# A unit's first value matmuls, one division piece and one background piece moved by half a step

## The chip, the cores and the metric

The kernel runs on one core of a Trainium2 chip. The metric is the device time of one execution in microseconds; the median of several runs is compared. The engines are named as in the profile: PE (TensorE matrix multiplies; PEld its weight loads), DVE (VectorE), ACT (ScalarE), POOL (GpSimd) and SP (SyncE, which issues the transfers).

## The reference

A decoder layer on x of 2 x 2048 x 512 in float32: self-attention of 16 heads of 32 with rotary positions, then attention to a context with a gelu in place of the softmax, then a feed-forward step with the signs of its weights, each after a layer norm and each added to x.

```python
def reference(x, ctx_1024, W_q, W_k, W_v, W_o, weights, scale, bias):
    def attn(x):
        Q, K, V = apply_rope(proj(W_q)), apply_rope(proj(W_k)), proj(W_v)
        scores = jnp.einsum('bhqd,bhkd->bhqk', Q, K) / jnp.sqrt(jnp.float32(DK))
        out = jnp.einsum('bhqk,bhkd->bhqd', jax.nn.softmax(scores, axis=-1), V)
        return out.transpose(0, 2, 1, 3).reshape(b, s, D) @ W_o.T
    def xattn(x, w1, w2):
        return jax.nn.gelu(x @ w1.T, approximate=True) @ w2
    def ffn(x):
        return jnp.clip((x @ sign(weights).T) * scale + bias, -100, 100)
    x = x + attn(_layernorm(x))
    x = x + xattn(_layernorm(x), ctx_1024, ctx_1024)
    x = x + ffn(_layernorm(x))
    return x
```

## The kernel before, in words

The two batches are worked through one after the other. For each, `project_batch` makes queries, keys and values, and `Attention.run` then does the attention, in which nearly all of the time goes by.

**Units and steps.** A unit is 256 queries of a group of four heads; a batch has 32 units (`NU`), and a block of 512 queries has eight of them. A unit has eight steps (`STEPS`), each over two of the 16 chunks of 128 keys, and a step has two half-steps: in the first, heads 0 and 1 are scored (`heads`) while the row maxima of heads 2 and 3 (`others`) are made for a unit eleven steps ahead (`AHEAD`); in the second the pairs change places.

**One half-step on each engine.** PE writes the scores of two heads, transposed, into their `st` banks (`scores`, L603; eight records a half-step, since each float32 matmul shows as two passes), and the scores for the maxima into two of the `ps` banks (`maxima`, L484; four records). A step's `st` is built on that of the step before: what is added is the product with the difference of two key blocks, so each head has one `st` bank for a whole unit. ACT makes the exponentials `pw` (L744), POOL adds those of the two key chunks to `sm` (L746), and DVE takes the row maxima out of `ps` (L496). At a unit's first step `lower` (L584) sets the `st` banks to the negated maxima first.

**Values and totals, one and two steps late.** `first_half` and `second_half` belong to the step before. `weigh` (L621) multiplies the `pw` of one key chunk with the values into the bank `acc`, eight records for four heads; `total` (L635) sums `sm` of the step before that into the same bank, eight records for half the queries. In step 0 of a unit the last values and totals of the unit before are made; the second half-step there also sums the last `sm`, for all 256 queries. In step 1 there are no totals. `ps_acc` has one bank, so the first `weigh` of a unit, at step 1, writes the bank that the unit before has used.

**The division** (`divide`) is a generator, one piece for each call of `finish`: a copy of `acc` to `num` by ACT (L649), at step 0's second half-step; the reciprocal of the first 128 totals by DVE (L655); the product of these by POOL (L658) and the second reciprocal; the second product. After the last piece of a block's last unit, `after_attention` is put into `queue` for that block.

**Background work.** `after_attention` is a generator of the output projection (L394), the context attention and the feed-forward step of one block. `background(1)` runs one piece at the end of each second half-step; `background(1, light=True)`, at each odd step's first half-step, runs one only if the piece is not marked heavy (a piece with matmuls or transposes). In a batch's last four units a piece is run in each first half-step, light or not. The background's PSUM tiles come out of `ps_s`.

**What sets the order.** In `run` the instructions of PE, DVE, ACT and POOL stay in the order in which the source issues them (`manual_schedule`); waits are put where tiles are shared. PSUM has eight banks: four in `ps_t` (the `st` of four heads), three in `ps_s` (the `ps` tiles in turn), one in `ps_acc`. DMAs of a unit's maxima go out on SP's queue and are not touched.

Of the kernel before, what the change touches and what calls it, by code (L numbers as in the profile page):

```python
# [36 lines left out]
def decoder_layer(  # L37
# [35 lines left out]
    def load_x(b, ch, pool=xpool):  # L73
        t = pool.tile([P, D], F32, tag="x", name=f"x_{b}_{ch}")
        nc.sync.dma_start(t, tokens(x[b], ch))
        return t
# [89 lines left out]
    def chunk_norm(ahead, b, ch, engine=nc.gpsimd):  # L166
        xc = ahead.pop(0)
        stats = stats_tile(1)
        chunk_stats(xc, stats[:, 0, 0:2])
        y, off = scale_and_shift(engine, stats)  # L170
        yield
        xn = work.tile([P, D], F32, tag="w", name="xn")
        nc.scalar.activation(xn, xc, AF.Identity, bias=off, scale=y)
        if ch + 2 < NCH:
            ahead.append(load_x(b, ch + 2))
        yield xn
# [5 lines left out]
    def turn(xn):  # L182
        pt = ps_t.tile([P, ND, P], F32, tag="t", name="pt")
        for i in range(ND):
            nc.tensor.transpose(pt[:, i, :], xn[:, i * P : (i + 1) * P], ident)  # L185
        xnt = work.tile([P, ND, P], F32, tag="w", name="xnt")
        nc.scalar.copy(xnt, pt)
        return xnt
# [243 lines left out]
    def background(n, light=False):  # L432
        while queue and n > 0 and not (light and heavy[0]):
            more = next(queue[0], queue)
            if more is queue:
                queue.pop(0)
                heavy[0] = False
            else:
                heavy[0] = more
                n -= 1  # L440
# [16 lines left out]
    class Attention:  # L457
# [227 lines left out]
        def run(self):  # L685
            prev = None
            sums_due = None
            ends = []

            def finish():  # L690
                while ends and next(ends[0], ends) is ends:
                    ends.pop(0)

            def first_half():
                if prev is not None:
                    self.weigh(prev, 0)
                if sums_due is not None:
                    self.total(sums_due, slice(0, P))

            def second_half():  # L700
                nonlocal sums_due
                if prev is not None:
                    self.weigh(prev, 1)
                if sums_due is not None:
                    self.total(sums_due, slice(P, HQ))
                sums_due = prev
                if prev is not None and prev[1] == STEPS - 1:
                    self.total(prev, slice(0, HQ))
                    ends.append(self.divide(prev[0]))
                    sums_due = None  # L710

            ordered = tc.manual_schedule(
                engines={
                    mybir.EngineType.PE,
                    mybir.EngineType.DVE,
                    mybir.EngineType.Activation,
                    mybir.EngineType.Pool,
                }
            )
            ordered.__enter__()  # L720
            attending.append(True)
            more = self.b + 1 < B
            for t in range(NU * STEPS):
                u, i = divmod(t, STEPS)
                if t == NU * STEPS - AHEAD:
                    free.append(True)
                if more and t == (NU - 1) * STEPS:
                    self.x_next = [load_x(self.b + 1, 0), load_x(self.b + 1, 1)]
                if more and t == NU * STEPS - STEPS // 2:
                    next_norm = chunk_norm(self.x_next, self.b + 1, 0)  # L730
                    next(next_norm)
                if more and t == NU * STEPS - 2:
                    xn = next(next_norm)
                pw = big.tile([P, 4, 2, HQ], F32, tag="s", name="pw")
                sm = sums.tile([P, 4, HQ], F32, tag="sm", name="sm")
                for heads, others in (((0, 1), (2, 3)), ((2, 3), (0, 1))):
                    if i == 0:
                        self.lower(u, heads)
                        self.wrap_around(self.units[u][1])
                    self.scores(u, i, heads, 0)  # L740
                    reduce = self.maxima(t + AHEAD, others)
                    self.scores(u, i, heads, 1)
                    for h in heads:
                        nc.scalar.activation(pw[:, h], self.st[h], AF.Exp, scale=SCALE)  # L744
                    hs = slice(heads[0], heads[1] + 1)
                    nc.gpsimd.tensor_add(sm[:, hs, :], pw[:, hs, 0, :], pw[:, hs, 1, :])  # L746
                    if reduce:
                        reduce()
                    if heads[0] == 0:
                        first_half()  # L750
                        finish()
                        if u >= NU - ND:
                            background(1)
                        elif t % 2 == 1:
                            background(1, light=True)
                    else:
                        finish()
                        second_half()
                        if prev is not None and prev[1] == STEPS - 1:
                            finish()  # L760
                        if (t + AHEAD) % STEPS == 0 and u + 1 < NU:
                            self.turn_maxima(u + 1)
                        if (t + AHEAD) % STEPS == STEPS - 1 and u + 1 < NU:
                            self.split_maxima(u + 1)
                        background(1)
                prev = (u, i, pw, sm)
            xnt = turn(xn) if more else None
            first_half()
            second_half()
            while ends:  # L770
                finish()
            attending.clear()
            free.clear()
            ordered.__exit__(None, None, None)
            return xnt
# [65 lines left out]
```

## Time and profile before

| what | us |
| --- | --- |
| median of three runs | 2694.99 (2693.69 to 2695.18) |
| the profiled execution | 2694.35 |
| its span, first to last instruction | 2692.6 |
| PE busy | 2666.4 (99%) |
| PEld busy | 1475.8 (55%) |
| POOL busy | 1762.9 (65%) |
| DVE busy | 1718.6 (64%) |
| ACT busy | 1323.3 (49%) |
| L496 row maxima, 2048 | 1309.1 in all, 0.682 each |
| L655 reciprocals, 128 | 120.6 in all, 0.943 each |
| L649 copies of `acc`, 64 | 37.6 in all, 0.587 each |

The attention of the first batch runs from 216 us to about 1326, that of the second from 1549 to about 2642. A unit without background work takes 30.91 us. The granted clock of PE is full in nearly all of the span.

A line of the timeline gives the start, the time until the last of the merged instructions ends, engine, line and operation, tiles (written <- read), shape and count, and in brackets how long the engine was idle before and what released it. Matmuls are pipelined and their ends are modelled: a PE that waits in the middle of a half-step can show as busy throughout, so their starts are what is to be compared.

### The profile page before, as it was taken

The numbers are of one execution on the slowest core, as the hardware profiler recorded it, in microseconds if no ns is written. First come the engines' busy times: TensorE is split into PE (matmuls) and PEld (weight loads), VectorE is DVE, ScalarE is ACT, GpSimd is POOL, SyncE is SP. The second block draws the span as 40 slices with busy tenths as digits, with TensorE's granted clock in tenths as the row PEclk, the third lists the DMA queues.
The fourth block names the chain that finished last, engine by engine and source line by source line (L and its number), as shares of the span: only waits on it lengthen the run. The fifth ranks groups of instructions, "written<-read, shape, count | busy, mean of one in ns | idle before, by whom it ended". The sixth has DMA issues, their size and how long they took to land.

```text
span 2692.6 us, 70762 instructions
## 1 busy us (share of the span) xinstructions
PE 2666.4 (99%) x30500; PEld 1475.8 (55%) x30500; DVE 1718.6 (64%) x2928; ACT 1323.3 (49%) x2394; POOL 1762.9 (65%) x1916
## 2 busy tenths in 40 slices
PE   8999999999999999999999999999999999999998
PEld 4445555555555555555554455555555555555555
DVE  3447777667766766676344477766767667766754
ACT  2214555455546554555422155555555455546553
POOL 3227777577857786777543287766787577857782
PEclk9999999999999999999999999999999999999999
DMA  3010000000000000000201000000000000000000
GB/s 126 24 32 2 3 2 2 2 2 18 18 2 2 10 26 2 2 10 25 76 24 40 5 2 3 2 3 2 2 26 10 2 2 18 18 2 2 18 18 17
DMA packets 36824, 40.65 MB, mean 15 GB/s; under 512 B 19206, under 2 KB 19718, under 8 KB 36512
## 3 DMA queue, kind: packets, MB, share of 16 engines
q1 hardware_dynamic: 36512, 36.14, 4.5%
q8 instruction: 239, 3.92, 0.6%
q14 instruction: 73, 0.60, 0.1%
HBM read 27.23 MB, written 8.90 MB: 13 GB/s over the span
## 4 chain that ended last, share of the span: by engine, by line
PE 98%; DVE 1%; DMA 0%; issue 0%; ACT 0%; SPq 0%; POOL 0%; POOLq 0%; ACTq 0%
PE st L603 24%; PE acc L621 22%; PE ps L484 18%; PE acc L635 8%; PE po L394 4%; PE pk L195 4%; PE pq L195 4%; PE pv L195 4%; PE pf L375 2%; PE st L584 2%; PE pt L357 1%; PE po L420 1%; PE ptqk L203 1%; PE ph L401 1%; PE pt L185 1%; DMA wk<-in_wk_t_dram 0%
## 5 line engine op out<-in xcount | busy, mean ns | idle before, releaser
L746 POOL TENSOR_TENSOR sm<-pw 128x512 f32<-128x512 f32 x1024 | 1297.9, 1274 | 567.4 <-ACT pw L744 563.1
L496 DVE TENSOR_REDUCE mx<-ps 128x1 f32<-128x512 f32 x2048 | 1309.1, 682 | 500.2 <-PE ps L484 498.3
L744 ACT ACTIVATE pw<-st 128x512 f32<-128x512 f32 x2048 | 1113.2, 596 | 942.0 <-PE ps L484 733.8
L484 PE MATMUL ps<-k,q 32*128 32x512 f32 x4096 | 1192.5, 639 | 1.5 <-DVE mx L496 1.5
L621 PE MATMUL acc<-pw,v 128*32 128x256 f32 x8192 | 655.0, 391 | 0.0
L635 PE MATMUL acc<-sm,ones 128*32 128x128 f32 x7680 | 388.3, 280 | 0.0
L621 PEld LDWEIGHTS acc<-pw,v 128*32 128x32 f32 x8192 | 161.9, 108 | 405.3 <-issue 386.9
L484 PEld LDWEIGHTS ps<-k,q 32*128 32x128 f32 x4096 | 356.8, 183 | 25.2 <-issue 13.7
L635 PEld LDWEIGHTS acc<-sm,ones 128*32 128x32 f32 x7680 | 247.2, 110 | 153.9
L603 PE MATMUL st<-q,dkk 32*128 32x256 f32 x2048 | 291.0, 400 | 0.0
L603 PE MATMUL st<-q,dkv 32*128 32x256 f32 x2048 | 289.9, 400 | 0.0
L603 PE MATMUL st<-q,dkq 32*128 32x256 f32 x2048 | 289.9, 400 | 0.0
L603 PEld LDWEIGHTS st<-q,dkk 32*128 32x128 f32 x2048 | 175.0, 184 | 89.5 <-issue 51.4
L603 PEld LDWEIGHTS st<-q,dkq 32*128 32x128 f32 x2048 | 172.7, 184 | 80.0 <-issue 54.2
L603 PEld LDWEIGHTS st<-q,dkv 32*128 32x128 f32 x2048 | 174.7, 184 | 58.9 <-issue 26.4
L231 POOL TENSOR_TENSOR r<-r 128x512 f32<-128x512 f32 x64 | 81.2, 1268 | 162.4 <-DVE r L230 150.6
L655 DVE RECIPROCAL num<-num 128x128 f32<-128x128 f32 x128 | 120.6, 943 | 54.2 <-ACT num L649 54.2
L603 PE MATMUL st<-q,wrap 32*128 32x256 f32 x1024 | 144.9, 400 | 0.0
L603 PE MATMUL st<-q,k 32*128 32x256 f32 x1024 | 133.2, 375 | 0.0
L149 DVE BATCH_NORM_STATS2 st<-x 128x6 f32<-128x512 f32 x96 | 65.4, 686 | 93.6 <-DMA x<-in_x_dram 93.2
L195 PE MATMUL pk<-wk,xnt 128*128 128x512 f32 x256 | 118.1, 605 | 3.4 <-DMA wk<-in_wk_t_dram 2.0
L394 PE MATMUL po<-wo,q 128*128 128x512 f32 x256 | 117.4, 603 | 0.0
(114 smaller groups left out, 1953.8 us busy)
## 6 DMA issues: line engine op xcount, KB each, us to landing
x<-in_x_dram SPq DMA_DIRECT2D x64, 256.0 KB
out_dram<-x SPq DMA_DIRECT2D x32, 256.0 KB
mrow<-rows SPq DMA_DIRECT2D x496, 0.8 KB
wk<-in_wk_t_dram SPq DMA_DIRECT2D x2, 1024.0 KB
wq<-in_wq_t_dram SPq DMA_DIRECT2D x2, 1024.0 KB
wv<-in_wv_t_dram SPq DMA_DIRECT2D x2, 1024.0 KB
wo<-in_wo_t_dram SPq DMA_DIRECT2D x1, 1024.0 KB
wf<-in_wf_t_dram SPq DMA_DIRECT2D x1, 1024.0 KB
```

Of the source, the lines that this page charges most:

```text
L149: nc.vector.bn_stats(st, xc)
L195: nc.tensor.matmul(dst, xnt[:, i, :], w[:, i, :], start=(i == 0), stop=(i == ND - 1))
L231: nc.gpsimd.tensor_add(r[:, 0, a], r[:, 0, a], r[:, 1, a])
L394: nc.tensor.matmul(ps, ot[:, i, cols], wo[:, i, :], start=(i == 0), stop=(i == ND - 1))
L484: nc.tensor.matmul(ps, self.q[qb][self.rows[h], g, q0 : q0 + P], self.k[kb][self.rows[h], g, :], start=True, stop=True,)
L496: nc.vector.tensor_reduce(mx[:, qc, h, kb : kb + 1], ps, AX.X, ALU.max)
L603: nc.tensor.matmul(self.st[h][:, c, :], keys[r, g, kc * P : (kc + 1) * P], self.q[qb][r, g, hf * HQ : (hf + 1) * HQ], start=False, stop=Tr ...
L621: nc.tensor.matmul(acc[self.rows[h], 0, :], self.v[self.chunk(i, c)][:, d0 : d0 + DK], pw[:, h, c, :], start=(i == 0 and c == 0), stop=(i ...
L635: nc.tensor.matmul(acc[self.rows[h], 1, part], ones, sm[:, h, part], start=False, stop=(i == STEPS - 1), skip_group_check=True,)
L655: nc.vector.reciprocal(num[:, 1, part], num[:, 1, part])
L744: nc.scalar.activation(pw[:, h], self.st[h], AF.Exp, scale=SCALE)
L746: nc.gpsimd.tensor_add(sm[:, hs, :], pw[:, hs, 0, :], pw[:, hs, 1, :])
```

## The change

At step 1 of each unit (`i == 1`) three things move. The value matmuls of the unit's first key chunk (`first_half`, which has no totals there) are issued in the second half-step, just ahead of those of the second chunk, and no longer in the first. The piece of the division that stood in the first half-step (the first reciprocal) is run in the second, and so each later piece half a step later than before. The light background piece of that first half-step is left out, and the queue goes on at the next place; in a batch's last four units, the piece in the first half-step stays.

```diff
                     if heads[0] == 0:
-                        first_half()
-                        finish()
+                        if i != 1:
+                            first_half()
+                            finish()
                         if u >= NU - ND:
                             background(1)
-                        elif t % 2 == 1:
+                        elif t % 2 == 1 and i != 1:
                             background(1, light=True)
                     else:
                         finish()
+                        if i == 1:
+                            first_half()
                         second_half()
```

## The prediction

> **What bounds the kernel now.** I read the page first, above all the shares of the chain that ended last; then the list of waits, and then the timelines of TensorE (PE) and VectorE (DVE) over one change of unit, since what the change moves lies there alone.
>
> ```profile
> PE 98%; DVE 1%; DMA 0%; issue 0%; ACT 0%; SPq 0%; POOL 0%; POOLq 0%; ACTq 0%
> PEld acc L621 <- ACT num L649: 17.7, 52, 0.3
> ```
>
> First line: the chain is PE's. The second is the wait behind which the moved values stand: the first value matmul (L621) of a unit needs the one `acc` bank, which ScalarE's copy (L649) gives free. It is 0.3 us at its longest and 17.7 us over 52 times, so 0.34 us each; but L621 stands idle for "issue" as long where no copy runs (386.9 us over 968 times, 0.40 each). It is what PE needs between score matmuls and value matmuls in any case, and I price this wait at nothing.
>
> I name half-steps by the step in the unit and a (heads 0, 1) or b (heads 2, 3); one begins at its first L603. PE in a change of unit without background work, with 1a at 718.61, 1b at 720.25, 2a at 722.15, 2b at 724.37 and 3a at 726.37:
>
> ```profile
> 718.61 0.48 PE L603 MATMUL st<-q,dkk 32*128 32x256 f32 x2
> ...
> 719.68 0.64 PE L621 MATMUL acc<-pw,v 128*32 128x256 f32 x8
> 720.25 0.48 PE L603 MATMUL st<-q,dkk 32*128 32x256 f32 x2
> 720.27 0.96 PE L484 MATMUL ps<-k,q 32*128 32x512 f32 x2
> ...
> 721.06 0.59 PE L484 MATMUL ps<-k,q 32*128 32x512 f32 x1
> 721.58 0.64 PE L621 MATMUL acc<-pw,v 128*32 128x256 f32 x8
> 722.15 0.48 PE L603 MATMUL st<-q,dkq 32*128 32x256 f32 x2
> ...
> 724.37 0.48 PE L603 MATMUL st<-q,dkq 32*128 32x256 f32 x2
> ...
> 726.37 0.48 PE L603 MATMUL st<-q,dkv 32*128 32x256 f32 x2
> ```
>
> DVE in the same stretch, the maxima (L496) and the two reciprocals (L655):
>
> ```profile
> 719.78 1.29 DVE L496 TENSOR_REDUCE mx<-ps 128x1 f32<-128x512 f32 x2 [1.11 <-PE ps L484]
> 720.99 0.94 DVE L655 RECIPROCAL num<-num 128x128 f32<-128x128 f32 x1
> 721.85 1.22 DVE L496 TENSOR_REDUCE mx<-ps 128x1 f32<-128x512 f32 x2
> 722.98 0.94 DVE L655 RECIPROCAL num<-num 128x128 f32<-128x128 f32 x1
> 723.84 1.22 DVE L496 TENSOR_REDUCE mx<-ps 128x1 f32<-128x512 f32 x2
> ```
>
> Elsewhere in the loop a half-step with totals takes 1.86 and 1.90 in turn. Without totals (1a) it takes 1.64. So 1b (1.90) is 0.26 over, 2a (2.22) 0.36 and 2b (2.00) 0.14: 0.76 us a unit of waits that "PE busy 99%" hides. Their cause is the `ps` banks: there are three, so the second L484 pair of a half-step waits until the first maximum of the half-step before is out. In 1b: the first maximum runs 719.78 to about 720.47 (a maximum has 0.68), the second bank is written from some 0.06 later, its second pass is at 721.06, and L621 comes 0.52 after that. In 2a and 2b the reciprocals have pushed the maxima back.
>
> The last view is the start of a batch, where no values exist yet and score half-steps follow one another:
>
> ```profile
> 219.55 0.59 PE L484 MATMUL ps<-k,q 32*128 32x512 f32 x1
> 220.06 0.71 PE L621 MATMUL acc<-pw,v 128*32 128x256 f32 x8
> ```
>
> ```profile
> 217.07 3.79 DVE L496 TENSOR_REDUCE mx<-ps 128x1 f32<-128x512 f32 x6 [1.23 <-PE ps L484]
> ```
>
> The three half-steps there begin at 216.12, 217.09 and 217.89: a half-step of scores alone costs PE 0.97 at most. But the maxima go on in a row, and the first L621 comes at 220.06, 2.17 after the start of its half-step where 1.07 is usual. What PE gains by leaving values out, it waits for at the banks.
>
> **The change part by part.**
>
> Wait on the copy: 0, from above.
>
> First values to 1b. 1a now costs 0.97, so 1b begins at about 719.59. Its second bank still waits for the maximum that starts at 719.78, because neither L484 nor L496 of 1a moves. The bank is free at 720.53 as before and L621 of 1b comes at 721.58 as before: the 0.66 gained in 1a is all waited for. Then eight L621 more follow. Their price: the last half-step of a unit's totals has eight 256-column L635 more than its neighbour, and 0.76 us (717.85 to 718.61) against 0.33 (715.88 to 716.21) from the first L635 to the next score; so +0.43. 2a begins at 722.58, not 722.15: **+0.43**. Queued behind L484's wait on PE are 1b's later scores, both value blocks and all that follows; ScalarE's exponentials wait for those scores, but end well ahead of the next use of their scores.
>
> Here two rules of the Trainium skill pull apart. "TensorEngine Tiling (Array Packing)", Tiling Modes, says that changing the tiling mode drains the array; one change less between scores and values speaks for the change, and by it alone the unit would gain about 0.1. "TensorE: Matmul & The Clock Gate", Part 2, says that matmuls stay in program order and only weight loads are pulled ahead; by it the values cannot pass the waiting L484, and the batch's start shows just that.
>
> First reciprocal to 1b, second to 2a. Maxima follow one another at 0.61, a reciprocal follows its maximum by 0.60, and the next maximum follows a reciprocal by 0.86 (720.99 to 721.85). In 1b the first maximum can start at 720.99, the second at about 721.69 (its bank's end), the reciprocal at 722.28 until 723.2. 2a's maxima are due 1.17 after 2a begins, 723.75: nothing is late. 2a takes 1.86, 2b begins at 724.44 and takes 1.90, as usual. The second reciprocal runs from 724.95; 2b's maxima, due at 725.61, start at 725.81 and the first ends at 726.44. 3a begins at 726.34 and its second bank waits until 726.49 instead of 726.36: +0.14. 3b begins at 728.34, before at 728.22; and 3b then has the shorter of the two turns. I take **+0.08** (0.02 to 0.15) for such a unit: +0.43, less the 0.36 and 0.14 of waits in 2a and 2b, plus 0.14 in 3a, and 0.01 to round.
>
> Where work in 1b hid the second reciprocal, nothing comes back. In the unit at 503.89 a projection (L394) from 511.58 takes 3.6 us, and 2a and 2b take 1.86 and 1.90 already: +0.43 + 0.14, and about 0.05 since the chunk statistics after 2b's maxima come later: **+0.6**. With four transposes (L357) in 1b, as in the unit at 539.24 (2a there is 2.22, 2b 1.86): +0.43 - 0.36 + 0.14 = **+0.2**.
>
> Light piece at 1a. Only three pieces in each query block of 512 find themselves there in quiet units; the rest of the time the next piece is heavy, or only waits its turn. They go to the next slots. The block's pieces end in the 15th unit, before the next block's first comes in the 17th: cost 0. If that slack were gone, a piece would cost what it costs elsewhere, so PE's work is the same. The moved scale-and-shift on POOL has a cover of a whole step, since totals use `sm` one step later. The divided queries (L658) are a half-step later; their first reader is a projection a step on. No DMA moves on SP's queue.
>
> By units: 37 without PE work at 1a to 2b, 37 x 0.08 = 3.0; 12 with a projection or context matmul in 1b, 12 x 0.6 = 7.2; 6 with transposes, 6 x 0.2 = 1.2; seven at the batches' ends, about +0.4 together (four at +0.2, two at -0.2 where no maxima are left, one at 0); the first unit of each batch, where 2a's wait of 0.25 goes and 2a begins no later, 2 x -0.2 = -0.4. Sum **+11.4**. The profiled execution took 2694.35 (span 2692.6), 0.6 under the median of 2694.99; +11.4 on either gives 2705.8 or 2706.4: **2706**. Its own bounds: 0.02 and 0.15 in the 37, half and one and a half in the 18 with background: +4 to +18, 2699 to 2713.
>
> **Rivals.**
>
> *The bank wait goes (faster).* If 1b's second bank were free when 1b begins, L621 would come at 719.59 + 1.07 = 720.66, and 2a 1.0 later, at 721.66: 0.49 before today's. With 2a and 2b free of waits the quiet unit gains 0.9, those with background 0.35: 37 x 0.9 + 18 x 0.35 = 40 us, 2655. It decides where 1a's first maximum ends before 719.6. For it: the drain rule and the short 1a. Against: that maximum starts at 719.78.
>
> *The reciprocals still push (slower).* If 2a and 2b keep their waits in spite of the longer 1b, the 0.43 is lost whole in 62 units: +27 us, 2721. For it: DVE has 2 x 0.94 us to place. Against: 2a's maxima come half a microsecond after the first reciprocal's end.
>
> *It cancels.* If units with background cost no more than quiet ones, 62 x 0.05 = 3 us: 2698, which is no change. For it: a projection of 3.6 us could hide some of the 0.43. Against: PE itself does both, one after the other.
>
> **How the numbers follow.** Forecast 0.62, cancelling 0.18, reciprocals 0.10, bank wait gone 0.10. A measurement here tells about 0.2%, 5.4 us, from no change. Of the forecast's 0.62 some 0.12 lies under that; of cancelling 0.16 is no change and 0.02 faster. So faster 0.12, same 0.28, slower 0.60. The range goes from 2695 to 2718: below it most of the first rival and a little of the third, above it most of the second.
>
> **What would show it.** In the timeline: 1a at 0.97, then L484's second pair of 1b at the same distance from the first maximum as now; sixteen L621 in a row; 2a at 1.86, 2b at 1.90, 3a near 2.00; a unit's length up by under 0.15 where quiet and by 0.5 to 0.6 with a projection in 1b. Wrong, if L621 of 1b comes earlier than 2.97 after 1a's start, if 2a stays over 1.9, or if the background pieces run into the next block.

## The result and the profile after

| | before | after |
| --- | --- | --- |
| median of eight runs, us | 2694.47 (2693.69 to 2695.18) | 2702.65 (2700.66 to 2704.77) |
| the profiled execution | 2694.35 | 2704.77 |
| its span | 2692.6 | 2703.0 |

The changed kernel is slower by 8.2 us, a ratio of 1.003 with a 95% interval of 1.0019 to 1.0041. It does the same work: 30500 matmul records, 2928 on DVE, 2394 on ACT and 1916 on POOL in both.

PE in the changed kernel at the change of unit that the prediction showed, now with 1a at 719.45 and 2a at 723.41; the columns are start, duration, engine, line, operation, tiles, shape, count:

```profile
719.45 0.48 PE L603 MATMUL st<-q,dkk 32*128 32x256 f32 x2
...
720.20 0.38 PE L603 MATMUL st<-q,dkk 32*128 32x256 f32 x2
720.41 0.59 PE L484 MATMUL ps<-k,q 32*128 32x512 f32 x1
720.42 0.60 PE L603 MATMUL st<-q,dkk 32*128 32x256 f32 x4
720.84 1.21 PE L484 MATMUL ps<-k,q 32*128 32x512 f32 x2
721.37 0.70 PE L603 MATMUL st<-q,dkk 32*128 32x256 f32 x4
721.89 0.59 PE L484 MATMUL ps<-k,q 32*128 32x512 f32 x1
722.41 1.07 PE L621 MATMUL acc<-pw,v 128*32 128x256 f32 x16
723.41 0.48 PE L603 MATMUL st<-q,dkq 32*128 32x256 f32 x2
...
725.27 0.48 PE L603 MATMUL st<-q,dkq 32*128 32x256 f32 x2
...
727.17 0.48 PE L603 MATMUL st<-q,dkv 32*128 32x256 f32 x2
```

1b begins at 720.42, only 0.97 after 1a. Its later scores start at 721.37, 0.95 after its first; 1a's last two start 0.75 after its first (719.45 to 720.20). L621 comes at 722.41: 2.96 after 1a by the rounded rows, which is where it was before (718.61 to 721.58, 2.97). Then there are sixteen in a row, and 2a begins 1.00 later and not 0.57. The row at 720.84 merges a record of the first maximum's matmul with the first of the second's, which shows best among the weight loads (PEld); in the brackets stand how long PEld was idle before and what released it:

```profile
721.36 0.18 PEld L484 LDWEIGHTS ps<-k,q 32*128 32x128 f32 x1 [0.74 <-DVE mx L496]
```

What stops 1b is on DVE:

```profile
720.62 2.60 DVE L496 TENSOR_REDUCE mx<-ps 128x1 f32<-128x512 f32 x4 [1.11 <-PE ps L484]
723.13 0.94 DVE L655 RECIPROCAL num<-num 128x128 f32<-128x128 f32 x1
724.58 1.29 DVE L496 TENSOR_REDUCE mx<-ps 128x1 f32<-128x512 f32 x2 [0.51 <-PE ps L484]
725.79 0.94 DVE L655 RECIPROCAL num<-num 128x128 f32<-128x128 f32 x1
726.65 1.22 DVE L496 TENSOR_REDUCE mx<-ps 128x1 f32<-128x512 f32 x2
```

1a's first maximum starts at 720.62, 1.17 after 1a as before, and is out some 0.7 later; until then 1b has only one free bank. Since PE now stands still long enough for it to show, the list of waits names the cause (us in all, times, longest us), before and after:

```profile
PEld ps L484 <- DVE mx L496: 7.0, 10, 1.6
```

```profile
PEld ps L484 <- DVE mx L496: 50.9, 70, 1.6
```

The list after also puts 44.3 us of L621's waits, 60 times, down to the exponentials (L744). In the unit shown that is not what L621 waits for: the last exponential before it ends at 721.85, and L621 comes 0.56 later, but 0.52 after the last L484 (721.89), as it did before (721.06 to 721.58). A kernel below, the faster of the two without 1a's maxima, has 43.6 us of the same waits, and there the change gains.

Half-steps of a quiet unit, from the starts of their first L603:

| | 1a | 1b | 2a | 2b | 3a | 3b | sum |
| --- | --- | --- | --- | --- | --- | --- | --- |
| before | 1.64 | 1.90 | 2.22 | 2.00 | 1.86 | 1.90 | 11.52 |
| after | 0.98 | 2.99 | 1.86 | 1.90 | 2.00 | 1.86 | 11.59 |

Summed over the units of both attention loops the trace after is 8.6 us longer: 3.9 in the first batch, 4.7 in the second. The remaining 1.9 us of the span lie in the projections and the tail. In the profiles of the kernels below this remainder goes from -1.0 to +1.5 (the one that is equal to the kernel before in its loops has 1.3), so I don't count it to the change; the medians differ by 8.2.

### The profile page after: what moved, and what is told of

Same layout as the page of the kernel before. It is cut to its first block, busy times and chain, and to the rows that moved or that the text cites. A ratio compares the mean times of both kernels' runs of the same rounds, so it can differ in the third digit from the quotient of the medians.

```text
span 2703.0 us, 70767 instructions
## 1 busy us (share of the span) xinstructions
PE 2677.7 (99%) x30500; PEld 1483.7 (55%) x30500; DVE 1726.1 (64%) x2928; ACT 1320.8 (49%) x2394; POOL 1760.5 (65%) x1916
## 4 chain that ended last, share of the span: by engine, by line
PE 98%; DVE 1%; issue 0%; DMA 0%; ACT 0%; POOL 0%; SPq 0%; POOLq 0%; ACTq 0%
PE st L603 24%; PE acc L621 22%; PE ps L484 19%; PE acc L635 8%; PE po L394 4%; PE pk L195 4%; PE pq L195 4%; PE pv L195 4%; PE pf L375 2%; PE st L584 2%; PE pt L357 1%; PE po L420 1%; PE ptqk L203 1%; PE ph L401 1%; PE pt L185 1%
## 5 line engine op out<-in xcount | busy, mean ns | idle before, releaser
L744 ACT ACTIVATE pw<-st 128x512 f32<-128x512 f32 x2048 | 1111.2, 595 | 950.5 <-PE ps L484 752.4
L484 PE MATMUL ps<-k,q 32*128 32x512 f32 x4096 | 1208.8, 638 | 1.5 <-DVE mx L496 1.5
L621 PE MATMUL acc<-pw,v 128*32 128x256 f32 x8192 | 641.6, 390 | 0.0
L484 PEld LDWEIGHTS ps<-k,q 32*128 32x128 f32 x4096 | 351.9, 183 | 69.1 <-DVE mx L496 50.9
L621 PEld LDWEIGHTS acc<-pw,v 128*32 128x32 f32 x8192 | 168.4, 108 | 387.7 <-issue 332.1
L603 PE MATMUL st<-q,dkq 32*128 32x256 f32 x2048 | 290.5, 400 | 0.0
L603 PE MATMUL st<-q,dkk 32*128 32x256 f32 x2048 | 290.0, 400 | 0.0
L603 PE MATMUL st<-q,dkv 32*128 32x256 f32 x2048 | 289.9, 400 | 0.0
L603 PEld LDWEIGHTS st<-q,dkq 32*128 32x128 f32 x2048 | 175.2, 184 | 81.6 <-ACT pw L744 37.9
L603 PEld LDWEIGHTS st<-q,dkv 32*128 32x128 f32 x2048 | 174.7, 184 | 58.7 <-issue 26.4
L603 PEld LDWEIGHTS st<-q,dkk 32*128 32x128 f32 x2048 | 163.8, 184 | 64.3 <-ACT pw L744 32.8
L603 PE MATMUL st<-q,wrap 32*128 32x256 f32 x1024 | 144.9, 400 | 0.0
L603 PE MATMUL st<-q,k 32*128 32x256 f32 x1024 | 133.2, 375 | 0.0
L149 DVE BATCH_NORM_STATS2 st<-x 128x6 f32<-128x512 f32 x96 | 65.4, 686 | 92.2 <-DMA x<-in_x_dram 91.9
L339 DVE TENSOR_TENSOR x<-po,x 128x512 f32<-128x512 f32 x64 | 44.2, 691 | 115.8 <-PE po L394 93.1
```

What stands on the lines that cost most here:

```text
L149: nc.vector.bn_stats(st, xc)
L484: nc.tensor.matmul(ps, self.q[qb][self.rows[h], g, q0 : q0 + P], self.k[kb][self.rows[h], g, :], start=True, stop=True,)
L603: nc.tensor.matmul(self.st[h][:, c, :], keys[r, g, kc * P : (kc + 1) * P], self.q[qb][r, g, hf * HQ : (hf + 1) * HQ], start=False, stop=Tr ...
L621: nc.tensor.matmul(acc[self.rows[h], 0, :], self.v[self.chunk(i, c)][:, d0 : d0 + DK], pw[:, h, c, :], start=(i == 0 and c == 0), stop=(i ...
```

## The experiments

All are the kernel before with an edit, but for one that edits the changed kernel. Sums per unit are again differences of the trace against that of before, from one unit's first L603 to the next's.

**The three parts alone.** The first moves the values and leaves the division and the light piece at 1a:

```diff
                     if heads[0] == 0:
-                        first_half()
+                        if i != 1:
+                            first_half()
                         finish()
...
                         finish()
+                        if i == 1:
+                            first_half()
                         second_half()
```

> Only the value matmuls move to 1b; the division and the light piece stay at 1a. My theory (1b's L621 is held by the ps bank, so the gain of 1a is waited for and the second value block adds 0.43, but the longer 1b takes the waits of 2a and 2b away): 1a 0.98, 1b 2.99, 2a 1.86, 2b 1.95, 3a 1.86, so +0.02 in each of 37 quiet units; +0.43 in 12 with a projection in 1b, where no wait was left to take away; +0.07 in 6 with transposes; -0.9 in the last unit of each batch and -0.2 in the first. Sum about +4, 2699 us. Rival (the move itself costs 0.43 in all 62 units, and the reciprocals' delay gives some of it back): +18 to +27, 2712 to 2721.

Measured: 2697.2 us (11 runs), ratio 1.0011, interval 1.0003 to 1.002. By units: 0.00 in most quiet ones, +0.43 in the 12 with a projection or context matmul in 1b, +0.09 with transposes, -0.9 in the last units, +3.7 for the loops together. Half-steps 1a to 2b are 0.98, 2.99, 1.86 and 1.93. So the theory held: the loss of 0.43 is there in 1b, and a quiet unit gets all of it back in 2a and 2b.

The second moves the division:

```diff
                         first_half()
-                        finish()
+                        if i != 1:
+                            finish()
```

> Only the division's pieces move by half a step; values and light piece stay at 1a. My theory: 2a's wait goes (2.22 to 1.86), 2b keeps 2.0 and 3a gets 2.0 as well: -0.22 in 37 quiet units, +0.13 in 12 with a projection in 1b, -0.2 in 6 with transposes: about -8, 2687 us. So it would be this half of the change that helps, and values and division would not add: +4 and -8 alone, +8 together, since both take away the same waits of 2a and 2b. Rival (the parts add): -8 less the values' part, so that the two sum to +8.

Measured: 2685.39 us (5 runs), ratio 0.9967, interval 0.9954 to 0.9979. By units: -0.26 in most quiet ones, +0.14 with a projection in 1b, -0.22 with transposes; -9.8 for the loops. DVE over a quiet change of unit in this kernel, with 1a at 402.51, 1b at 404.15 and 2a at 406.05:

```profile
403.68 1.29 DVE L496 TENSOR_REDUCE mx<-ps 128x1 f32<-128x512 f32 x2 [1.11 <-PE ps L484]
405.32 1.29 DVE L496 TENSOR_REDUCE mx<-ps 128x1 f32<-128x512 f32 x2 [0.35 <-PE ps L484]
406.53 0.94 DVE L655 RECIPROCAL num<-num 128x128 f32<-128x128 f32 x1
```

With no reciprocal between the first two pairs, 1b's first maximum is out at 406.0, when 2a begins, and 2a's wait of 0.36 is gone. What the parts do alone, +2.7 and -9.1, is -6.4 together; both in one kernel give +8.2. They do not add, because each takes 2a's wait away by another road, and it can go only once. Once the values have moved, the division's move has no wait of 2a left to remove and brings 3a's 0.14: the two kernels' loops differ by 8.6 - 3.7 = 4.9 us.

The third leaves out the light piece alone:

```diff
-                        elif t % 2 == 1:
+                        elif t % 2 == 1 and i != 1:
                             background(1, light=True)
```

> Only the light background piece at 1a is left to the next slot. Theory: 0, 2694.5 within 1 us, and the background's end stays in the same unit. Rival (the background is what the change disturbs): most of the +8 is here.

Measured: 2694.16 us (11 runs), ratio 0.9999, interval 0.999 to 1.0008; the loops are shorter by 0.5 us. No cost of the piece can be told from zero.

**The bank wait itself.** Two kernels, that of before and the changed one, in which 1a makes no maxima:

```diff
+                nc.vector.memset(self.mx[u][:, 1, 2:4, 0:1], -1e30)
...
-                    reduce = self.maxima(t + AHEAD, others)
+                    reduce = None
+                    if i != 1 or heads[0]:
+                        reduce = self.maxima(t + AHEAD, others)
```

> The kernel before without the row maxima of 1a: the two score products and two maxima of that half-step are left out, and their columns (first key block, second 128 queries, heads 2 and 3) are set low once a unit, so the shift of the exponent comes from three key blocks there. Theory (bank wait): 1b falls from 1.90 to 1.64, a wait of 0.25 comes at 2a instead: about -0.36 a quiet unit, some -15 us in all, 2680. It is the base for the run beside it.

> The changed kernel without the row maxima of 1a, as in the run beside it. Theory (what the change gains at 1a is waited for at 1b's second ps bank, which hangs on 1a's first maximum): with no maximum in 1a there is nothing to wait for, 2a begins about 3.0 after 1a instead of 3.97, and the change turns from a loss into a gain: about 0.47 a quiet unit, 0.1 with background, 0.9 in the last units, some 21 us faster than the run beside it (15 to 28). Rival (the second value block in a row, or the longer 1b itself, costs the 0.43, whatever the banks do): 8 us or more slower than the run beside it, as with the maxima.

Measured: 2674.71 us without the change and 2640.83 with it (4 runs each, on one chip); ratios to the kernel before of 0.9928 (0.9914 to 0.9941) and 0.9803 (0.979 to 0.9817). The change that cost 8 us gains 33.9 where 1a holds no maximum. That excludes the rival, by which the loss would stay whatever the banks do. PE from 1a to 2a in the two, first without the change and then with it (here scores are L604, the maxima's matmuls L485, values L622, the maxima L497):

```profile
369.98 1.13 PE L604 MATMUL st<-q,dkk 32*128 32x256 f32 x8
...
373.25 0.48 PE L604 MATMUL st<-q,dkq 32*128 32x256 f32 x2
```

```profile
367.67 1.25 PE L604 MATMUL st<-q,dkk 32*128 32x256 f32 x16
368.63 1.02 PE L485 MATMUL ps<-k,q 32*128 32x512 f32 x4
369.59 1.07 PE L622 MATMUL acc<-pw,v 128*32 128x256 f32 x16
370.59 0.48 PE L604 MATMUL st<-q,dkq 32*128 32x256 f32 x2
```

2a begins 2.92 after 1a, against 3.27 in the kernel beside it. Sixteen value matmuls take 1.00 to the next score (369.59 to 370.59), as they do with the maxima; what is gone is the wait, and in this kernel's list it is back at the size of before:

```profile
PEld ps L485 <- DVE mx L497: 7.1, 11, 1.6
```

I had expected a gain of 15 to 28: a quiet unit gains 0.60 and not 0.47, one with a projection 0.21 and not 0.1. Part of it is the first line: with nothing else in 1a, the scores of heads 2 and 3 run beside those of heads 0 and 1, which I had not counted. One after the other, 0.97 + 1.07 + 1.00 would be 3.04 to 2a and not 2.92. So, as an estimate, 0.12 a unit or 7 of the 33.9 us come from this and not from the bank.

**A version that beats both.** If the division's place is what pays, its pieces can be put apart. The next kernel leaves all values at 1a and runs the pieces in second half-steps only:

```diff
                         first_half()
-                        finish()
```

> Values stay at 1a; the division's pieces run in second half-steps alone, so the copy is at 0b, the reciprocals at 1b and 2b, the products at 2b and 3b, and the block's background starts one step later. Theory: DVE catches up by 0.6 in each half-step, so a reciprocal (0.94) late by 0.14 at most where two are a step apart: 2a 1.86, 2b 2.0, 3a 1.86: -0.36 in quiet units, +0.12 where a projection hid it, -0.2 with transposes: about -13, 2681 us, faster than both kernels. Rival (a wait of the reciprocals is only put off): no more than e2 gives, 2687.

Measured: 2688.04 us (10 runs), ratio 0.9975, interval 0.9966 to 0.9985; half of the gain that I expected. Most quiet units have -0.36 as expected (six, in which a block's background begins, have -0.66); the units with a projection in 1b have +0.81, not +0.12. DVE there, with 2b at 513.07, 3a at 514.97 and 3b at 516.83:

```profile
514.24 1.29 DVE L496 TENSOR_REDUCE mx<-ps 128x1 f32<-128x512 f32 x2 [0.57 <-PE ps L484]
515.45 0.94 DVE L655 RECIPROCAL num<-num 128x128 f32<-128x128 f32 x1
516.31 0.64 DVE L149 BATCH_NORM_STATS2 st<-x 128x6 f32<-128x512 f32 x1
516.98 0.18 DVE L150 BATCH_NORM_AGGREGATE stats<-st 128x2 f32<-128x6 f32 x1
517.08 2.56 DVE L496 TENSOR_REDUCE mx<-ps 128x1 f32<-128x512 f32 x4
```

The reciprocal and the chunk statistics of the projection (L149, L150) stand behind the same maxima, and 3a's maxima start at 517.08, 2.11 after 3a began, where 1.17 is usual; 3b takes 2.80 where it took 1.99. So these units keep the old places, where the projection hides both reciprocals. Whether 1b will hold heavy work is known when the source runs:

```diff
                         first_half()
-                        finish()
+                        if i == 1 and heavy[0]:
+                            finish()
```

> As e4 (pieces of the division in second half-steps, reciprocals at 1b and 2b), but where the background's next piece at 1a is heavy, so that 1b will hold a projection or transposes, the first reciprocal stays at 1a and the second at 1b. Theory: e4's +0.81 in the 12 units with a projection in 1b is the second reciprocal and the chunk statistics in one half-step (2b), and goes; its -0.22 in the 6 with transposes goes as well; quiet units keep -0.36. e4's loops were -7.2 together, so -7.2 - 9.8 + 1.3 = -15.7, 2679 us. Rival (e4's loss comes from the block's later start, not from the reciprocal): no better than e4, 2688.

Measured: 2678.56 us (5 runs), ratio 0.9943, interval 0.9929 to 0.9957: 15 us under the kernel before and some 24 under the changed one. By units: -0.36 in most quiet ones (-0.66 in the same six as above), 0.00 where 1b holds a projection or transposes; the loops together -15.2. A block's background starts a step later here too (its first projection is at 4b in both kernels, at 3b before), so it was not the later start that cost 0.81. Its DVE at a quiet change of unit:

```profile
403.65 1.29 DVE L496 TENSOR_REDUCE mx<-ps 128x1 f32<-128x512 f32 x2 [0.35 <-PE ps L484]
404.86 0.94 DVE L655 RECIPROCAL num<-num 128x128 f32<-128x128 f32 x1
405.72 1.22 DVE L496 TENSOR_REDUCE mx<-ps 128x1 f32<-128x512 f32 x2
407.41 1.29 DVE L496 TENSOR_REDUCE mx<-ps 128x1 f32<-128x512 f32 x2 [0.47 <-PE ps L484]
408.61 0.94 DVE L655 RECIPROCAL num<-num 128x128 f32<-128x128 f32 x1
```

Between the reciprocals there is a pair of maxima for which DVE waits again (idle 0.47 before 407.41): it has caught up, and the second reciprocal finds no delay to add to.

## Why the prediction was right

**The wait on the copy, at 0.** It held, as far as the traces go. In the last unit of each batch there is neither maximum nor total in step 1, and in the trace before 1a, behind the copy, and 1b, with no copy near, take the same 1.63. No kernel was run that takes this wait away alone.

**First values to 1b, +0.43.** Right in mechanism and size. L621 of 1b stays 2.96 to 2.97 after 1a, and 2a begins 3.96 after it, not 3.54. The two kernels without 1a's maxima show that the bank is the reason.

**The reciprocals.** 2a 1.86, 2b 1.90 and 3a 2.00 were forecast and measured. Most quiet units got longer by 0.07 to 0.08 (forecast 0.08), one with a projection by 0.57 (0.6), one with transposes by 0.21 (0.2).

**The light piece, 0.** Right, by the run that leaves it out alone.

**The sum.** 11.4 was forecast, the loops have 8.6 (2706 us, against 2702.65 measured). The step that was mis-sized is the seven units at the batches' ends: "four at +0.2, two at -0.2 where no maxima are left, one at 0". The last unit of each batch has -0.91, since without maxima the scores of all four heads run side by side. The other five are -0.04, -0.05, +0.06, +0.43 and -0.39: the four at +0.2 hold together +0.4 instead of +0.8, and the one at 0 is -0.39. That is -1.8 for the seven where I had +0.4, 2.2 of the 2.8 that the sum was off. The sum's own lower bound has a slip, too: 0.02 in the 37 and half of the 8.4 in the 18 make +4.9, not +4.

**The two rules.** The trace fits the drain that the Trainium skill names in "TensorEngine Tiling (Array Packing)", Tiling Modes: a score half-step without values is followed after 0.97, one with values needs 1.07 until the first of them. No run shows that this 0.1 is the drain. Of what one change less would give, nothing arrives, as the values stay behind the waiting maximum's matmul. There the rule on the program's order gave the right forecast. As it stands in the Trainium skill, "TensorE: Matmul & The Clock Gate", Part 2, that matmuls stay in program order, it says more than the traces bear out; the last section has the starts that differ.

**The rivals.** The bank wait did not go by itself; taken away by hand, the change gains 34 us (the two kernels without 1a's maxima), so that rival's mechanism was sound and its condition not met. The reciprocals did not keep pushing: 2a and 2b are at 1.86 and 1.90. And the loss does not cancel where 1b holds a projection.

## What to carry to other kernels

Where an engine shows as 99% busy, compare the lengths of equal stretches rather than its busy share: 0.76 us a unit lay hidden here. Work that is moved out of a stretch which ends in a wait for a buffer leaves a hole, not a gain, so ask first what the next stretch waits for. And two moves that remove the same wait must each be tried alone: one of them may be all gain and the other all cost.

## What the runs showed of the hardware

With nothing between them, the scores of two pairs of heads cost as little as those of one. Each head's scores read 32 partitions of their own; that they overlap for this reason was not tested by itself. PE in the last unit of the second batch in the changed kernel, which makes no maxima:

```profile
2628.13 1.16 PE L603 MATMUL st<-q,dkk 32*128 32x256 f32 x16
2629.22 1.07 PE L621 MATMUL acc<-pw,v 128*32 128x256 f32 x16
```

Sixteen score records take 1.09 until the first L621; in the kernel before, eight take 1.06 there (2618.30 to 2619.36). I had priced two half-steps of scores one after the other, at 0.97 each.

Starts on PE need not follow the order of issue. In the view of the changed kernel without 1a's maxima, all sixteen scores of 1a and 1b start before the first L485, at 368.63, though `run` issues 1b's last scores (heads 2 and 3) behind these matmuls for the maxima of heads 0 and 1. But a matmul that waits holds back what is issued after it: in the changed kernel 1b's last scores go into banks that 1b has begun to fill already, and yet start only at 721.37, just behind the L484 that waited until 721.36.
